# Seven block products for eight in the up projections of the second layer

## The chip, the cores and the metric

The kernel runs on one core of a Trainium2 chip. The metric is the time of one execution in device microseconds (us). The kernel before takes 371.68 us, the median of three runs (371.5 to 371.9).

## The reference

The input `x` is [4, 512, 256] in float32: four batches of 512 tokens with 256 features. Two layers follow each other. Each normalizes `x`, computes a mixer `s` and a gated feed-forward network on the normalized input, and adds `s * silu(ffn)` to `x`. The matrices of the network are `W1` and `W3` [1024, 256] and `W2` [256, 1024].

```python
x = L0_attn_x
xn = _layernorm(x, axis=-1)
s = _L0_attn_ref(xn, ...)            # a product with two small matrices, an RMS norm
g = _silu(_L0_ffn_ref(xn, W1, W2, W3))
x = x + s * g
xn = _layernorm(x, axis=-1)
s = _L1_attn_ref(xn, ...)            # layer norm, causal attention with one head of 256
g = _silu(_L1_ffn_ref(xn, W1, W2, W3))
x = x + s * g

def ffn(x, W1, W2, W3):
    up_gate = einsum('bsd,hd->bsh', x, W1)
    up_lin  = einsum('bsd,hd->bsh', x, W3)
    hidden  = fwht(silu(up_gate) * up_lin)     # a Hadamard transform, a constant matrix
    return einsum('bsh,dh->bsd', hidden, W2)
```

The two einsums with `W1` and `W3` are the up products of which the change speaks.

## The kernel before

Every float32 operand of a large product is held as two float32r tiles, a high part (a rounded copy made by ScalarE) and a low part (the rest, a subtraction on VectorE); the helper `split` (L59 to L62) issues the two. A product is then the sum of three: high by high, low by high and high by low (`mm3`, L64 to L71), all accumulated in one bank of PSUM. Activations are transposed first, so that features lie on partitions; `xTs[layer, b]` holds the pair (high, low), each [128, 2 halves of features, 512 tokens].

The first layer runs over the four batches with `ffn("f0_b")`, and the second with `ffn("f1_b")`; in the profile they appear as `f_0` to `f_3`, both layers under the same names. In `ffn` the 1024 hidden units come in eight chunks `c` of 128. For each chunk there are two banks of tag `gu` (three exist), one for the gate and one for the linear product: 2 x 6 matmuls with 512 moving columns (L411). Then come `silu` on ScalarE (L423), the multiplication on VectorE (L424), a `split` of the result, and with a delay of one chunk the `down` products (L382): 4 tiles of 128 tokens x 3 matmuls with 256 moving columns. Weights `w13` are loaded and split once per layer, in four pairs `q` of two chunks each (`load_w13`, `split_w13`); those of the second layer at L758.

`Beside` interleaves other work: between the parts of a chunk `ffn` calls `slot`, and there the next steps of a list of generators are issued: the gating of the batch before (`gate`), the normalization of the next batch (`norm`), the attention of this batch and the first six steps of that of the next. `attention(b)` begins with the transposition of the normalized input into two banks of tag `ms` (three exist); from these two banks it makes `xTs[1, b]` for the network (L500) and the input of attention itself (L499 to L506).

The Tile framework puts the semaphores in and orders each engine's instructions at build time, from its own estimate of times, with the order of the program as priority. On the chip every engine's queue is executed in that order. All loads of weights and inputs and all stores are issued from SyncE's queue (`SPq`).

Pools of buffers that the change touches: `w13h`, `w13l` (4 each), `xt` (4), `w2` (4), `t4` (10 of [128, 1024]), `hid` (14 of [128, 512]).

## Time and profile before

| | |
|---|---|
| time, median of 3 runs | 371.68 us (371.5 to 371.9) |
| the profiled execution, its own time | 372.08 us |
| its span, first to last instruction | 370.3 us |
| granted TensorE clock | 1.00 |
| TensorE matmul busy | 362.9 us, 98% |
| VectorE busy | 245.7 us, 66% |
| ScalarE busy | 180.1 us, 49% |
| DMA | 15.50 MB, mean 42 GB/s |

The profiled execution is one run; it took 0.40 us more than the median. The profile's views used here are the page with its sums, the timeline of an engine (start, duration, engine, line, operation, tiles), the waits (who waited for whom, in us), the windows (busy time of each engine in a stretch, in the order PE, PEld, DVE, ACT, POOL, then granted clock, DMA share and GB/s) and the list of DMA issues (size and us from issue to landing). PE is TensorE, PEld its weight loads, DVE is VectorE, ACT is ScalarE, SPq SyncE's queue.

### The profile page before, as it was taken

The numbers are of one execution on the slowest core, as the hardware profiler recorded it, in microseconds if no ns is written. First come the engines' busy times: TensorE is split into PE (matmuls) and PEld (weight loads), VectorE is DVE, ScalarE is ACT, GpSimd is POOL, SyncE is SP. The second block draws the span as 40 slices with busy tenths as digits, with TensorE's granted clock in tenths as the row PEclk, the third lists the DMA queues.
The fourth block names the chain that finished last, engine by engine and source line by source line (L and its number), as shares of the span: only waits on it lengthen the run. The fifth ranks groups of instructions, "written<-read, shape, count | busy, mean of one in ns | idle before, by whom it ended". The sixth has DMA issues, their size and how long they took to land.

```text
span 370.3 us, 5487 instructions
## 1 busy us (share of the span) xinstructions
PE 362.9 (98%) x2173; PEld 320.0 (86%) x2173; DVE 245.7 (66%) x520; ACT 180.1 (49%) x332; POOL 18.6 (5%) x22
## 2 busy tenths in 40 slices
PE   7999999999999999999999999999999999999995
PEld 5777998888988898889898998988989899888895
DVE  5998468994539949945958576474774467475543
ACT  3646426163453335545563654274563656366621
POOL 1000111100011102100011000010000000000000
PEclk9999999999999999999999999999999999999999
DMA  7916000300000004110100001100011000010001
GB/s 228 331 60 227 3 0 2 113 0 2 0 2 1 0 19 153 58 57 2 59 2 0 0 2 57 59 0 3 0 58 47 12 0 1 2 57 2 1 2 57
DMA packets 9369, 15.50 MB, mean 42 GB/s; under 512 B 864, under 2 KB 7168, under 8 KB 9344
## 3 DMA queue, kind: packets, MB, share of 16 engines
q1 hardware_dynamic: 9056, 14.90, 12.0%
q8 instruction: 17, 0.28, 0.3%
q10 hardware_dynamic: 288, 0.26, 0.2%
q14 instruction: 8, 0.07, 0.1%
HBM read 13.04 MB, written 2.11 MB: 41 GB/s over the span
## 4 chain that ended last, share of the span: by engine, by line
PE 90%; DVE 3%; DMA 2%; SPq 1%; issue 1%; ACT 1%
PE f_2gu L70 12%; PE f_3gu L70 12%; PE f_1gu L70 12%; PE f_0gu L70 7%; PE f_0dn L382 6%; PE f_2dn L382 6%; PE f_3dn L382 6%; PE f_1dn L382 6%; PE sc L70 4%; PE pv L70 4%; PE o L70 3%; PE v L70 3%; PE tq L70 3%; DMA w13raw<-in_w 2%; PE pt L560 1%; PE mps L170 1%
## 5 line engine op out<-in xcount | busy, mean ns | idle before, releaser
L70 PE MATMUL f_1gu<-xtl,w13h 128*128 128x512 f32 x64 | 25.4, 396 | 0.0
L70 PE MATMUL f_2gu<-xth,w13l 128*128 128x512 f32 x64 | 25.4, 396 | 0.0
L70 PE MATMUL f_3gu<-xtl,w13h 128*128 128x512 f32 x64 | 25.3, 396 | 0.0
L70 PE MATMUL f_2gu<-xtl,w13h 128*128 128x512 f32 x64 | 25.3, 396 | 0.0
L70 PE MATMUL f_1gu<-xth,w13l 128*128 128x512 f32 x64 | 25.3, 396 | 0.0
L70 PE MATMUL f_3gu<-xth,w13l 128*128 128x512 f32 x64 | 25.2, 396 | 0.0
L70 PE MATMUL f_0gu<-xtl,w13h 128*128 128x512 f32 x60 | 23.7, 395 | 0.0
L70 PE MATMUL f_0gu<-xth,w13l 128*128 128x512 f32 x60 | 23.2, 395 | 0.0
L61 ACT CAST f_1hh<-f_1h 128x512 fp32r<-128x512 f32 x16 | 9.9, 621 | 22.4 <-DVE f_1h L424 22.4
L70 PE MATMUL f_3gu<-xth,w13h 128*128 128x512 f32 x64 | 20.7, 400 | 0.0
L70 PE MATMUL f_2gu<-xth,w13h 128*128 128x512 f32 x64 | 20.7, 397 | 0.0
L70 PE MATMUL f_1gu<-xth,w13h 128*128 128x512 f32 x64 | 20.6, 395 | 0.0
L70 PE MATMUL f_0gu<-xth,w13h 128*128 128x512 f32 x60 | 19.7, 410 | 0.6 <-ACT f_0h L423 0.6
L61 ACT CAST f_2hh<-f_2h 128x512 fp32r<-128x512 f32 x16 | 9.9, 619 | 20.2 <-DVE f_2h L424 20.2
L424 DVE TENSOR_TENSOR f_3h<-f_3h,f_3gu 128x512 f32<-128x512 f32 x16 | 11.0, 686 | 10.8 <-PE f_3gu L70 9.5
L382 PE MATMUL f_1dn<-w2h,f_1hh 128*128 128x256 f32 x64 | 17.8, 287 | 0.0
L382 PE MATMUL f_1dn<-w2l,f_1hh 128*128 128x256 f32 x64 | 17.7, 284 | 0.0
L382 PE MATMUL f_3dn<-w2l,f_3hh 128*128 128x256 f32 x64 | 17.7, 281 | 0.0
L382 PE MATMUL f_3dn<-w2h,f_3hh 128*128 128x256 f32 x64 | 17.6, 281 | 0.0
L382 PE MATMUL f_2dn<-w2h,f_2hh 128*128 128x256 f32 x64 | 17.6, 283 | 0.0
L382 PE MATMUL f_2dn<-w2l,f_2hh 128*128 128x256 f32 x64 | 17.5, 281 | 0.0
L424 DVE TENSOR_TENSOR f_2h<-f_2h,f_2gu 128x512 f32<-128x512 f32 x16 | 10.9, 681 | 9.5 <-PE f_2gu L70 8.0
(239 smaller groups left out, 1087.7 us busy)
## 6 DMA issues: line engine op xcount, KB each, us to landing
w13raw<-in_w SPq DMA_DIRECT2D x7, 512.0 KB, 6.1
w2raw<-in_w SPq DMA_DIRECT2D x4, 512.0 KB, 5.4
mrb<-there SPq DMA_DIRECT2D x4, 512.0 KB, 3.7
x<-in_x SPq DMA_DIRECT2D x3, 512.0 KB, 3.3
out<-x SPq DMA_DIRECT2D x6, 256.0 KB, 2.1
w13raw<-in_w SPq DMA_DIRECT2D x2, 256.0 KB, 5.2
wout<-in_w_outT SPq DMA_DIRECT2D x1, 512.0 KB, 9.0
win<-in_w_in SPq DMA_DIRECT2D x1, 512.0 KB, 8.7
```

The costliest lines, as they stand in the source:

```text
L61: h = nc.scalar.copy(hi, src)
L70: ins = nc.tensor.matmul(o, l, r, start=n == 0, stop=n == len(seq) - 1)
L170: nc.tensor.matmul(o[:, i, :], lhsT(k, i), rhs(k), start=k == 0, stop=k == nk - 1)
L382: return nc.tensor.matmul(o, l[:, sl(t)], r[:, c, :], start=start, stop=stop, skip_group_check=True)
L424: gates.append(nc.vector.tensor_tensor(h, h, gu[1], ALU.mult))
L560: nc.tensor.transpose(pt[:, sl(j)], p[:, sl(j)], ident)
```

## The change

The first layer's computation stays. In the second layer the up products of a group `q` (256 hidden units, gate and linear) are read as a product of two 2x2 block matrices: the weights' blocks are (linear, gate) by (first, second half of the features), those of the input (first, second half of the features) by (late, early half of the tokens). Strassen's algorithm in Winograd's form needs seven block products in place of eight, with sums of blocks: S1 to S4 of the weights, T1 to T4 of the input.

- `ffn_s` takes the place of `ffn` for `f1_b`. A group has three banks, `gate_`, `lin` and `z`. Each block product is 6 matmuls with 256 moving columns. Partial results are added by letting further products accumulate on a bank, by three copies on ScalarE (`gate_` into `lin`, `z` into `h1`, `gate_` into `v`) and two additions on VectorE. The down products follow with a delay of one group.
- `prep_s` loads the second layer's raw weights, forms S1 to S4 on VectorE, splits the seven blocks and writes high and low parts to DRAM, 896 KB each per group. It runs beside the first layer's batches 2 (three groups) and 3 (one).
- `load_s` brings the seven blocks of a group back, high and low, for each of the 16 groups of the second layer. Four buffers hold two groups; the load of the next group is issued when a group begins. The resident pairs of L758 are gone.
- `attention` makes the blocks of the input (`t_blocks`): sums T1 to T4 on VectorE, and splits of seven blocks of 256 columns, where before it split two of 512.

The core of the diff (unchanged lines and the code that only gathers buffers are cut):

```diff
@@ split_w13 / norm @@
-        hi = wp.tile([P, 2, S], F32R, tag="w13h", name=f"w13h_{layer}_{q}", bufs=4)
-        lo = wp.tile([P, 2, S], F32R, tag="w13l", name=f"w13l_{layer}_{q}", bufs=4)
+        both = wp.tile([P, 2, 2, S], F32R, tag="w13", name=f"w13_{layer}_{q}", bufs=4)
+        hi, lo = both[:, 0], both[:, 1]
...
+    A11, A12, A22, S1, S2, S3, S4 = range(7)
+    B11, B22, B21, T1, T2, T3, T4 = range(7)
+    sdram = {}
+    def prep_s(q):
+        raw = t4(f"sraw{q}", [P, 4, D])
+        nc.sync.dma_start(raw, a["w13_1"][q])
+        yield
+        sums = t4(f"ssum{q}", [P, 4, D])
...
+        nc.vector.tensor_tensor(s1, a21, a22, ALU.add)
+        nc.vector.tensor_tensor(s3, a11, a21, ALU.subtract)
+        nc.vector.tensor_tensor(s2, s1, a11, ALU.subtract)
+        nc.vector.tensor_tensor(s4, a12, s2, ALU.subtract)
+        yield
+        sdram[q] = there = [
+            dram.tile([P, 7, D], F32, tag=f"s{i}", name=f"s{i}_{q}", bufs=4) for i in range(2)
+        ]
+        for at, n, src in ((0, 3, raw), (3, 4, sums)):
+            parts = [t4(f"sp{at}_{i}_{q}", [P, n, D], F32R) for i in range(2)]
+            split(src[:, :n, :], *parts)
+            for i in range(2):
+                nc.sync.dma_start(there[i][:, at : at + n, :], parts[i].bitcast(F32))
+            yield
+    def load_s(q, n):
+        parts = [
+            wp.tile([P, 7, D], F32R, tag="w13", name=f"sw{i}_{n}_{q}", bufs=4) for i in range(2)
+        ]
+        for i in range(2):
+            nc.sync.dma_start(parts[i].bitcast(F32), sdram[q][i])
+        return parts
...
@@ ffn_s @@
+        for q in range(NH // 2):
+            wh, wl = pairs(q)
+            def product(o, i, j, begin=False, end=False):
+                head = None
+                seq = [(wh, xh), (wl, xh), (wh, xl)]
+                for n, (w, x) in enumerate(seq):
+                    for c in range(2):
+                        with after(head if n == 0 else None):
+                            ins = nc.tensor.matmul(
+                                o[:, c, :], w[:, i, sl(c)], x[j],
+                                start=begin and n + c == 0, stop=end and n == 2,
+                                skip_group_check=True,
+                            )
...
+            gate_, lin = bank(f"{q}g"), None
+            product(gate_, A11, B11, begin=True)
+            lin = bank(f"{q}l")
+            nc.scalar.copy(lin, gate_)
+            z = bank(f"{q}z")
+            product(z, S1, T1, begin=True)
+            h1 = hid(f"{name}h1_{q}").rearrange("p (c n) -> p c n", c=2)
+            nc.scalar.copy(h1, z)
+            slot(4 * q)
+            product(gate_, S2, T2)
+            v = hid(f"{name}v{q}").rearrange("p (c n) -> p c n", c=2)
+            nc.scalar.copy(v, gate_)
+            product(z, S4, B22, end=True)
+            nc.vector.tensor_tensor(v, z, v, ALU.add)
+            slot(4 * q + 1)
+            product(gate_, S3, T3)
+            nc.vector.tensor_tensor(h1, gate_, h1, ALU.add)
+            product(lin, A12, B21, end=True)
+            slot(4 * q + 2)
+            product(gate_, A22, T4, end=True)
+            nc.scalar.activation(h1, h1, AF.Silu)
+            nc.vector.tensor_tensor(h1, h1, v, ALU.mult)
...
+            parts(0, h1)
+            h0 = hid(f"{name}h0_{q}").rearrange("p (c n) -> p c n", c=2)
+            nc.scalar.activation(h0, gate_, AF.Silu)
+            nc.vector.tensor_tensor(h0, h0, lin, ALU.mult)
+            parts(1, h0)
+            queue.append((q, hs))
+            if len(queue) > (1 if last is None else 2):
+                down(*queue.pop(0))
+            slot(4 * q + 3)
...
@@ attention @@
+        os_ = [transpose_half(f"xt1_{b}", xn, k) for k in range(2)]
+        early, late = slice(0, D), slice(D, S)
...
+        b1, b2 = os_
+        nc.scalar.copy(b12, b1[:, early])
+        nc.vector.tensor_tensor(ts_[0], b12, b1[:, late], ALU.subtract)
+        split(b1[:, late], ...)
+        nc.vector.tensor_tensor(ts_[2], b2[:, early], b12, ALU.subtract)
+        nc.vector.tensor_tensor(fs[0], b1, mrb[:, 0, :], ALU.subtract)
+        nc.vector.tensor_tensor(ts_[1], b2[:, early], ts_[0], ALU.subtract)
+        nc.vector.tensor_tensor(ts_[3], b2[:, late], ts_[1], ALU.subtract)
+        split(back, *tb2x)
+        nc.vector.tensor_tensor(fs[1], b2, mrb[:, 0, :], ALU.subtract)
+        split(sums, *tt)
         for k in range(2):
-            o = transpose_half(f"xt1_{b}", xn, k)
-            f = t2(f"xf{b}_{k}", [P, S])
-            nc.vector.tensor_tensor(f, o, mrb[:, 0, :], ALU.subtract)
-            split(o, xh[:, k, :], xl[:, k, :])
+            f = fs[k]
             nc.vector.tensor_tensor(f, f, mrb[:, 1, :], ALU.mult)
...
@@ the loops over batches @@
         if b == 2:
             tasks.append((norm(1, 0), NORM))
+            tasks += [(prep_s(q), 4) for q in range(3)]
         if b == 3:
+            tasks.append((prep_s(3), 4))
...
-    w13_1 = [split_w13(1, q, load_w13(1, q)) for q in range(4)]
+    def pairs(b):
+        def one(q):
+            for n in range(4 * b + q, min(4 * b + q + 2, 16)):
+                if n not in loaded:
+                    loaded[n] = load_s(n % 4, n)
+            return loaded[4 * b + q]
+        return one
...
-            dn = ffn(f"f1_{b}", xTs[1, b], w13_1.__getitem__, w2_1, bg.slot)
+            dn = ffn_s(f"f1_{b}", xTs[1, b], pairs(b), w2_1, bg.slot)
```

More of the change, by code (lines that the diff above doesn't have):

```diff
@@ L271, with xt_pair @@
     xns, xTs, mrs = {}, {}, {}
+    def xt_pair(name):
+        both = act.tile([P, 2, 2, S], F32R, tag="xt", name=name, bufs=2)
+        return both[:, 0], both[:, 1]
+    A11, A12, A22, S1, S2, S3, S4 = range(7)
[6 more added lines that the diff above has]
+        sums = t4(f"ssum{q}", [P, 4, D])
+        a11, a12, a22, a21 = (raw[:, i, :] for i in range(4))
+        s1, s2, s3, s4 = (sums[:, i, :] for i in range(4))
+        nc.vector.tensor_tensor(s1, a21, a22, ALU.add)
[12 more added lines that the diff above has]
+            yield
@@ new lines, in load_s, with t_blocks @@
+    def load_s(q, n):
[5 more added lines that the diff above has]
+        return parts
+    def t_blocks(b):
+        if b % 2:
+            whole = [w2_tile(f"tb{i}_{b}") for i in range(2)]
+        else:
+            whole = [
+                act.tile([P, NH, D], F32R, tag="xt", name=f"tb{i}_{b}", bufs=2)
+                for i in range(2 if b else 1)
+            ]
+        parts = [[w[:, i, :] for i in range(7)] for w in whole]
+        if len(parts) < 2:
+            lo3, lo4 = t4(f"tb3_{b}", [P, 3, D], F32R), t4(f"tb4_{b}", [P, 4, D], F32R)
+            whole = [whole[0], None]
+            parts.append([lo3[:, i, :] for i in range(3)] + [lo4[:, i, :] for i in range(4)])
+            return parts, [(whole[0][:, 0, :], lo3[:, 0, :]),
+                           (whole[0][:, 1:3, :], lo3[:, 1:3, :]),
+                           (whole[0][:, 3:7, :], lo4)]
+        return parts, [tuple(w[:, i:j, :] for w in whole) for i, j in ((0, 1), (1, 3), (3, 7))]
@@ L273, in norm_first @@
     def norm_first():
         xn = act.tile([P, NT, D], F32, tag="xn", name="xn0_0", bufs=3)
-        hi = act.tile([P, 2, S], F32R, tag="xt", name="xth0_0", bufs=4)
-        lo = act.tile([P, 2, S], F32R, tag="xt", name="xtl0_0", bufs=4)
-        xns[0, 0], xTs[0, 0] = xn, (hi, lo)
+        hi, lo = xTs[0, 0] = xt_pair("xt0_0")
+        xns[0, 0] = xn
         x = xs[0]
@@ L326, in norm @@
         xn = act.tile([P, NT, D], F32, tag="xn", name=f"xn{layer}_{b}", bufs=3)
-        hi = act.tile([P, 2, S], F32R, tag="xt", name=f"xth{layer}_{b}", bufs=4)
-        lo = act.tile([P, 2, S], F32R, tag="xt", name=f"xtl{layer}_{b}", bufs=4)
-        xns[layer, b], xTs[layer, b] = xn, (hi, lo)
+        xns[layer, b] = xn
         with after(first["gate"] if layer == 0 and b > 1 else None):
@@ L351, in norm @@
             return
+        hi, lo = xTs[0, b] = xt_pair(f"xt0_{b}")
         for k in range(2):
-            o = transpose_half(f"xt{layer}_{b}", xn, k)
+            o = transpose_half(f"xt0_{b}", xn, k)
             split(o, hi[:, k, :], lo[:, k, :])
@@ L454, in ffn, with ffn_s, down, bank @@
         return None
+    def ffn_s(name, blocks, pairs, w2, slot, last=None):
+        w2h, w2l = w2
+        xh, xl = blocks
+        if last is None:
+            dn = [psum(f"{name}dn{i}", [P, 2, D], tag="dn", bufs=2) for i in range(2)]
+            outs = [dn[t // 2][:, t % 2, :] for t in range(NT)]
+        else:
+            outs = [psum(f"{name}dn{t}", [P, D], **DN[t // 2]) for t in range(NT)]
+        firsts = {}
+        def down(q, hs, tiles=range(NT)):
+            for c in range(2):
+                for t in tiles:
+                    hh, hl = (h[:, c, sl(t % 2)] for h in hs[t // 2])
+                    o = outs[t]
+                    for n, (l, r) in enumerate(((hh, w2h), (hh, w2l), (hl, w2h))):
+                        head = q + c + n == 0
+                        stop = q == NH // 2 - 1 and c == 1 and n == 2
+                        own = head and (t % 2 == 0 or last is not None)
+                        with after(firsts[t // 2] if head and not own else None):
+                            ins = nc.tensor.matmul(
+                                o, l, r[:, 2 * q + c, :], start=own, stop=stop, skip_group_check=True
+                            )
+                        if own:
+                            firsts[t // 2] = ins
+            return ins
+        def bank(n):
+            return psum(f"{name}gu{n}", [P, 2, D], tag="gu", bufs=3)
+        queue = []
+        for q in range(NH // 2):
[4 more added lines that the diff above has]
+                for n, (w, x) in enumerate(seq):
+                    for c in range(2):
+                        with after(head if n == 0 else None):
+                            ins = nc.tensor.matmul(
+                                o[:, c, :], w[:, i, sl(c)], x[j],
+                                start=begin and n + c == 0, stop=end and n == 2,
+                                skip_group_check=True,
+                            )
+                        if head is None:
+                            head = ins
+            gate_, lin = bank(f"{q}g"), None
[20 more added lines that the diff above has]
+            nc.vector.tensor_tensor(h1, h1, v, ALU.mult)
+            hs = []
+            def parts(i, h):
+                hh, hl = (
+                    hid(f"{name}h{p}{i}_{q}", F32R).rearrange("p (c n) -> p c n", c=2) for p in "hl"
+                )
+                split(h, hh, hl)
+                hs.append((hh, hl))
+            parts(0, h1)
[7 more added lines that the diff above has]
+            slot(4 * q + 3)
+        if last is None:
+            for e in queue:
+                down(*e)
+            return dn
+        (q0, q1), ts_ = queue, range(NT)
+        order = [(q0, ts_[:2])] + [(q1, ts_[t : t + 1]) for t in (0, 1)]
+        order += [(q, ts_[t : t + 1]) for t in (2, 3) for q in (q0, q1)]
+        ins = None
+        for q, tiles in order:
+            with after(ins):
+                ins = down(*q, tiles)
+            if q is q1:
+                last(tiles[0], outs[tiles[0]])
+        return None
@@ L493, in attention @@
         xn, wqk, wvo = xns[1, b], first["wqk"], first["wvo"]
-        (xh, xl), mrb = xTs[1, b], mrs[b]
+        mrb = mrs[b]
+        xTs[1, b], (tb11, tb2x, tt) = t_blocks(b)
         xg = gh, gl = t4(f"xgh{b}", [P, 2, S], F32R), t4(f"xgl{b}", [P, 2, S], F32R)
+        os_ = [transpose_half(f"xt1_{b}", xn, k) for k in range(2)]
+        early, late = slice(0, D), slice(D, S)
+        sums = t4(f"tsum{b}", [P, 4, D])
+        ts_ = [sums[:, i, :] for i in range(4)]
+        back = os_[1].rearrange("p (h n) -> p h n", h=2)
+        b1, b2 = os_
+        b12 = t2(f"b12_{b}", [P, D])
+        nc.scalar.copy(b12, b1[:, early])
+        nc.vector.tensor_tensor(ts_[0], b12, b1[:, late], ALU.subtract)
+        split(b1[:, late], tb11[0].rearrange("p a n -> p (a n)") if len(tb11[0].shape) > 2 else tb11[0],
+              tb11[1].rearrange("p a n -> p (a n)") if len(tb11[1].shape) > 2 else tb11[1])
+        nc.vector.tensor_tensor(ts_[2], b2[:, early], b12, ALU.subtract)
+        fs = [t2(f"xf{b}_{k}", [P, S]) for k in range(2)]
+        nc.vector.tensor_tensor(fs[0], b1, mrb[:, 0, :], ALU.subtract)
[4 more added lines that the diff above has]
+        split(sums, *tt)
         for k in range(2):
-            o = transpose_half(f"xt1_{b}", xn, k)
-            f = t2(f"xf{b}_{k}", [P, S])
-            nc.vector.tensor_tensor(f, o, mrb[:, 0, :], ALU.subtract)
-            split(o, xh[:, k, :], xl[:, k, :])
+            f = fs[k]
             nc.vector.tensor_tensor(f, f, mrb[:, 1, :], ALU.mult)
@@ L756, in gate_tile @@
         nc.sync.dma_start(out[B - 1, sl(t), :], x)
-    w13_1 = [split_w13(1, q, load_w13(1, q)) for q in range(4)]
+    loaded = {}
+    def pairs(b):
[5 more added lines that the diff above has]
+        return one
     for b in range(B):
@@ L773 @@
         if b + 1 < B:
-            dn = ffn(f"f1_{b}", xTs[1, b], w13_1.__getitem__, w2_1, bg.slot)
+            dn = ffn_s(f"f1_{b}", xTs[1, b], pairs(b), w2_1, bg.slot)
             bg.finish()
         else:
-            ffn(f"f1_{b}", xTs[1, b], w13_1.__getitem__, w2_1, bg.slot, 4, last=gate_tile)
+            ffn_s(f"f1_{b}", xTs[1, b], pairs(b), w2_1, bg.slot, last=gate_tile)
 def _rows(w):
@@ L788, in _w13, with _w31 @@
     return w.reshape(2, P, 4, S).transpose(2, 1, 0, 3)
+def _w31(w1, w3):
+    g, l = (w.T.reshape(2, P, 4, D) for w in (w1, w3))
+    return np.stack([l[0], l[1], g[1], g[0]], axis=2).transpose(1, 0, 2, 3)
 def _w2(w2):
@@ L822 @@
     for n in range(2):
-        arrays[f"w13_{n}"] = _w13(v[f"L{n}_ffn_W1"], v[f"L{n}_ffn_W3"])
+        arrays[f"w13_{n}"] = (_w31 if n else _w13)(v[f"L{n}_ffn_W1"], v[f"L{n}_ffn_W3"])
         arrays[f"w2_{n}"] = _w2(v[f"L{n}_ffn_W2"])
```

## The prediction

> **What bounds the kernel now.** I read the page's sums first, then the waits of TensorE, then its timeline.

> ```profile
> PE 362.9 (98%) x2173; PEld 320.0 (86%) x2173; DVE 245.7 (66%) x520; ACT 180.1 (49%) x332; POOL 18.6 (5%) x22
> ```

> ```profile
> PE warm L648 <- DVE zr L643: 1.5, 1, 1.5
> PE mps L170 <- ACT wg L198: 0.7, 1, 0.7
> PE f_0gu L70 <- ACT f_0h L423: 0.6, 1, 0.6
> PE f_0gu L417 <- ACT xth L314: 0.4, 1, 0.4
> ```

> TensorE is busy 98% of the span, and the four lines of the second view are all its waits: 3.2 us, all in the first 40 us. Busy time can hide gaps between pipelined matmuls, so the spacing of starts is what I use:

> ```profile
> 168.94 0.28 PE L382 MATMUL f_3dn<-w2h,f_3hh 128*128 128x256 f32 x1
> ...
> 170.35 0.63 PE L70 MATMUL f_3gu<-xth,w13h 128*128 128x512 f32 x2
> ...
> 173.14 0.28 PE L70 MATMUL v<-wvoh,xgh 128*128 128x256 f32 x1
> ```

> Between the first two stand 12 matmuls with 256 columns: 1.41 us, 0.1175 each. Between the second and third stand 12 with 512: 2.79 us, 0.2325 each. TensorE issues without gaps at a time proportional to columns. The second layer runs from about 176 to 366 us; two of its batches by the windows:

> ```profile
> 220.60:269.34 48.74, 48.74 (x303) 43.58 (x302) 30.97 (x68) 25.52 (x46) 2.34 (x2) 1.00 0.07 22
> 269.34:318.00 48.66, 48.66 (x297) 43.21 (x296) 29.93 (x56) 26.33 (x47) 0.00 (x0) 1.00 0.07 23
> ```

> A batch takes 48.7 us, all of it TensorE: 96 x 0.2325 = 22.3 up, 96 x 0.1175 = 11.3 down, and 15.1 of attention. VectorE is busy 62 to 64%, ScalarE 52 to 54%. So less work on TensorE shortens the kernel, as long as the other two can follow.

> **What is removed on TensorE.** A group has 24 matmuls of 512 columns now, 24 x 0.2325 = 5.58 us, and 7 x 6 = 42 of 256 after, 42 x 0.1175 = 4.94. That is 0.645 us less, and over 16 groups 10.3 us. The weights change at every matmul in both forms; the down products do so too at 0.1175, so weight loading adds nothing. [...]

> **ScalarE and VectorE in a group.** Added per group: three copies of [128, 512] on ScalarE and two additions on VectorE (4 and 4 operations of 512 columns become 7 and 6). The nearest rows are casts out of PSUM of 512 columns at 0.59 and additions at 0.69. No row has ScalarE writing PSUM, as `gate_` into `lin` does; I bound it by 0.37 (a 256-column cast) and 0.82 (the slowest 512-column activation, `xg`), and take 0.60, the cast reading the same PSUM. [...] Per batch this is 12 x 0.60 = 7.2 us on ScalarE and 8 x 0.69 = 5.5 on VectorE.

> **The blocks of the input.** ScalarE now casts 2 x 0.59 = 1.2 us per batch; after, 0.37 + 0.37 + 0.59 + 1.05 = 2.4. VectorE has 4 x 0.68 = 2.7; after, five operations of 256 columns at 0.42, three of 512 at 0.68 and one of 1024 at 1.22 make 5.4. The prices of 256 and 1024 columns come from

> ```profile
> L61 ACT CAST w13h<-w13raw 128x1024 fp32r<-128x1024 f32 x7 | 7.4, 1051 | 2.0 <-DMA w13raw<-in_w 2.0
> L62 DVE TENSOR_TENSOR w13l<-w13raw,w13h 128x1024 fp32r<-128x1024 f32 x7 | 8.4, 1217 | 0.0
> L754 DVE TENSOR_TENSOR gl<-gl,xn 128x256 f32<-128x256 f32 x4 | 1.6, 426 | 2.6 <-ACT gl L753 2.4
> ```

> In all, ScalarE goes from 26 to 34.5 us and VectorE from 30.5 to 38.7 us in a batch of 48.7 - 2.6 = 46.1: 75% and 84%. Neither becomes the bound by its sum. The question is waiting.

> **The new waits on TensorE.** Now a bank goes from TensorE to ScalarE once. After, `gate_` goes there and back: the second product on it waits for the copy into `lin`, the third for the copy into `v`, the fourth for VectorE's addition; the second on `z` waits for the copy into `h1`. Four handovers per group, 64 in all, each with the rest of the group, its down products and then the next group queued behind it. A product issues in 6 x 0.1175 = 0.71; its last result lands 0.28 after its start, 0.16 late; a copy takes 0.60. So the second product on `gate_` can start 0.76 us after the first has issued, and the product between them covers 0.71. Three of the four handovers also have a `slot` in between, 15.1 / 16 = 0.94 us of attention on average, and the 24 down products of the group before, 2.82 us, can be ordered into a gap. Cover is short only where ScalarE is away for long, in each softmax:

> ```profile
> 289.90 1.28 ACT L549 ACT_TABLE_LOAD   x1
> ...
> 293.65 1.28 ACT L423 ACT_TABLE_LOAD   x1
> 294.94 0.60 ACT L423 ACTIVATE f_2h<-f_2gu 128x512 f32<-128x512 f32 x1
> ```

> Two table loads with exponentials between them hold ScalarE for up to 5.04 us; copies queued behind wait. Of this 0.61 and 0.27 are casts, so about 4.2. Against 2.82 + 0.94 = 3.76 of cover, some 0.4 us stays open, eight times: 3.2 us. The ends are 0 (the order of the program puts the copies elsewhere) and 1.2 us in each of 16 groups, two handovers each late by one 0.6 us operation: 19.2 us. I take 3.2 because today's trace has the same blocks with ScalarE and shows TensorE no wait in them.

> **The turn of a batch.** This is where it is tight already:

> ```profile
> 264.91 1.04 PE L258 MATMUL xt_2tp<-ident,xn 128*128 128x128 f32 x8
> 268.66 0.58 ACT L61 CAST xth<-xt_2tp 128x512 fp32r<-128x512 f32 x1
> 269.34 0.86 PE L70 MATMUL f_2gu<-xth,w13h 128*128 128x512 f32 x3
> ```

> The first up product starts 0.1 us after the second cast ends; down products and attention filled the 3.4 us before it exactly. VectorE has no gap there from 265.4 to 273.7. The change puts 2.7 us of block sums and 1.2 of additions more into it, and T1, which the second product needs, comes from the last split. Against these 3.9 us stand 12 more down products held back (1.41), and the first and sixth product, 2 x 0.71, which need only early blocks. Left are about 1.0 us; part goes into the following group, so I take 0.8 at each of three turns, 2.4 us, with ends 0 and 3.9 x 3 = 11.7.

> **Streaming the weights.** A group needs 2 x 896 KB, 1.84 MB, each in about 11.5 us: 160 GB/s.

> ```profile
> w13raw<-in_w SPq DMA_DIRECT2D x7, 512.0 KB, 6.1
> x<-in_x SPq DMA_DIRECT2D x3, 512.0 KB, 3.3
> ```

> 3.5 loads of 512 KB at 3.3 us in a row are 11.6 us; at the 331 GB/s of the page's second slice they take 5.5. A load waits for the last product of the group before and is needed a group later. With a group's seven products spread over about 8.5 of its 11.5 us that leaves 14.5 us; in the last batch, whose late groups have little attention, 7.8 + 1.2 = 9. So I cost it at nothing, the cover being one whole group of products; if the cover is gone, it costs up to 2.6 us for each of the last two groups. In SyncE's queue a load can stand behind the transposed moments (`there`, then `mrb`, which waits for it): 1.3 us between their issues now, inside the same slack. Loads also write SBUF beside the engines; subtractions (L62, 512 columns) took 0.68 us at 10 to 22 us, with DMA at 78%, as they do later, so I take nothing.

> **Preparing the sums, the end.** `prep_s` puts per group 4 x 0.42 + 0.93 + 1.22 = 3.8 us on VectorE and 1.85 on ScalarE, beside 98 to 176 us, where they are busy 55.0 and 35.6 of 78.3 us; the four splits at 172 to 180 (1.22 and 1.05 each) go. Cost nothing, hidden by TensorE's own work there; without that cover, 4 x (3.8 - 1.2) = 10.4 us of VectorE. At the end the same 48 down products cover the last chunk's chain: nothing.

> **The sum.** From the profiled execution, 372.08 (span 370.3 and 1.8 around it): -10.3 + 3.2 + 2.4 = 367.4. That run was 0.40 above the median, so 367.0 by the median.

> **The rivals.** *All waits are covered*: 372.1 - 10.3 - 0.4 = 361.4. For it: no wait of TensorE in the second layer today. Against: VectorE at 84%, and the turn.

> *The handovers pace the groups* (the other side): ScalarE's in-order queue holds the copies behind attention's casts and softmax, each group is late by 1.2 us, 19.2 in all: 372.1 - 10.3 + 19.2 - 0.4 = 380.6. It decides from 10.3 / 16 = 0.645 us per group, one operation of ScalarE or VectorE ahead of one handover. For it: the loop gate, copy, gate, copy, gate, addition, gate alone takes 4 x 0.71 + 3 x 0.16 + 0.60 x 2 + 0.69 = 5.2 us of 11.5, and three operations ahead (3 x 0.65) and a softmax (4.2) bring it to 11.4, the group's whole time. Against: the down products wait for nothing in it.

> *The stream comes late*: the second end above, 2 x 2.6 us, on top of my sum: 372.2, no change. For it: 3.3 us per 512 KB today. Against: 331 GB/s when loads are queued.

> That the seven products are not fewer can't be: 43,008 columns per batch against 49,152.

> **Chances.** All covered 0.2; my forecast, 363.5 to 370.9, 0.36, which gives 367.0; no change 0.05 (within 0.2%, 0.74 us, is about what a measurement of this kernel can't tell from none); paced by handovers 0.39, of which a quarter lies above 383. So faster 0.56, same 0.05, slower 0.39, and the range 361.4 to 383.0; the forecast's own is 363.5 to 370.9.

> **What would show it.** Right: 168 up matmuls of 256 columns per batch, 0.1175 apart; batches of 46 to 48 us; TensorE's waits in the second layer 3 to 8 us in sum, named on ScalarE's copies near table loads and on the block splits at the turns; every weight load landed before its first product. Wrong: waits of TensorE on `lin`, `h1`, `v` in most groups (second rival); waits on DMA (third); a spacing above 0.1175 or a granted clock under 1.00 while the stream runs, which no row of this trace can exclude.

## The result and the profile after

The changed kernel takes 398.98 us, the median of four runs (397.1 to 401.08), against 371.79 for the kernel before beside it: 1.0734 times as long, with a 95% interval of 1.0679 to 1.0788. It is 27.2 us slower where 4.7 us less was predicted, and lies above the range. The profiled execution took 401.08 us, its span is 399.3.

The sums and the clock on its page:

```profile
PE 369.2 (92%) x2461; PEld 335.7 (84%) x2461; DVE 280.5 (70%) x592; ACT 212.3 (53%) x392; POOL 18.9 (5%) x22
...
PEclk9999999999999999968999999999999999989998
```

TensorE fell from 98% to 92% of a longer span; VectorE and ScalarE are far from full. The clock row is below 9 from 170 to 190 us, near 355 us and in the last slice; in the kernel before it is not. Was the saving there at all? Two rows of TensorE's timeline, in the middle of the second layer:

```profile
270.78 0.87 PE L565 MATMUL f_1gu2z<-tb,sw 128*128 128x256 f32 x6
271.49 0.28 PE L70 MATMUL pv<-vh,pl 128*128 128x256 f32 x1
```

Six matmuls of 256 columns issue in 0.71 us, as predicted. I added up all spacings of starts in both traces. Spacings at their undisturbed length (0.2325 us for 512 columns, 0.1175 for 256 and so on) sum to 356.8 us before and 346.5 after: the 10.3 us are saved in full. What lies above that length at full clock (the gaps) went from 12.0 to 41.4 us, and another 9.6 us lie in the stretches at half clock. -10.3 + 29.4 + 9.6 = 28.7, and the span grew by 29.0. So nearly everything that went wrong is waiting and clock. Not all of the 9.6 us is the clock itself, because two gaps of 1.2 and 1.5 us lie in these stretches; some 7 us are left for it, an estimate. Who waited, by the waits of TensorE:

```profile
PE pt L750 <- ACT p L739: 3.8, 4, 1.2
PE f_3dn L543 <- ACT f_3hh L61: 2.9, 3, 1.1
PE pv L70 <- ACT ph L61: 2.3, 2, 1.1
PE f_3dn L448 <- DVE f_3hl L62: 1.7, 1, 1.7
PE f_0gu0z L565 <- ACT f_0h L580: 1.7, 1, 1.7
```

No line of this view names a DMA. Of 112 block products only 10 waited for 0.4 us or more, 7.7 us in all; the largest sum is that of `pt`, the transposes of attention's exponentials `p`, an operation that the change doesn't touch. By stage the spacings above their length are 11.9 us at 160 to 200 us, the passage between the layers (6.4 of it at half clock), 16.7 from 200 to 340, and 14.0 from 340 to the end.

**The passage.** Windows of 10 us (columns as in the prediction):

```profile
160.00:170.00 10.00, 9.48 (x56) 8.03 (x54) 9.72 (x32) 4.82 (x14) 1.93 (x2) 1.00 0.88 310
170.00:180.00 10.00, 6.59 (x30) 6.01 (x30) 8.11 (x17) 3.65 (x6) 1.72 (x1) 0.66 0.47 188
180.00:190.00 10.00, 8.14 (x43) 7.01 (x42) 8.18 (x13) 5.96 (x11) 0.00 (x0) 0.83 0.00 0
```

In the kernel before, TensorE is busy for all of these 30 us at clock 1.00 and VectorE for 4.6, 7.1 and 7.4 of 10. Now VectorE is full from 160 to 170 us, and TensorE, which needs its results, starves from 170 us on. Only about 2 us of that is the preparation itself. More is the normalization for the second layer (`norm`), which starts on VectorE at 160.96 us; before, it started at 141.47. The timeline of SyncE's queue tells why the preparation is so late:

```profile
130.69 0.35 SPq L411 DMA_DIRECT2D mrb<-there  x1
131.13 0.37 SPq L294 DMA_DIRECT2D sraw<-in_w  x1
...
158.34 0.38 SPq L294 DMA_DIRECT2D sraw<-in_w  x1
```

The first load of `prep_s` stands right behind the moments of the normalization (`there` at 129.31 us, `mrb`), which wait for their rows until then; the others follow at intervals of 9 us, the last at 158.34. So all the preparation falls into 131 to 175 us, and its last part into the passage. VectorE's timeline shows both ends:

```profile
132.27 0.69 DVE L490 TENSOR_TENSOR f_2h<-f_2h,f_2gu 128x512 f32<-128x512 f32 x1 [4.01 <-PE f_2gu L70]
...
172.93 1.22 DVE L62 TENSOR_TENSOR sp<-ssum,sp 128x1024 fp32r<-128x1024 f32 x1
174.07 0.42 DVE L678 TENSOR_TENSOR tsum<-b,xt_0tp 128x256 f32<-128x256 f32 x1
```

It was idle for 4 us just before, and the last split of the preparation runs directly ahead of the first block sum of the input, for which TensorE waits.

**A softmax.** Timeline of all engines, last batch:

```profile
347.67 0.87 PE L565 MATMUL f_3gu1g<-tb,sw 128*128 128x256 f32 x6
...
348.38 0.87 PE L565 MATMUL f_3gu0g<-tb,sw 128*128 128x256 f32 x6
...
350.10 1.28 ACT L739 ACT_TABLE_LOAD   x1
...
351.90 1.08 PE L750 MATMUL pt<-ident,p 128*128 128x128 f32 x3 [1.03 <-ACT p L739]
```

and the same place of the last batch in the kernel before, where scores end and transposes begin (TensorE and ScalarE):

```profile
332.27 1.28 ACT L549 ACT_TABLE_LOAD   x1
...
332.53 0.28 PE L70 MATMUL sc<-xgh,tql 128*128 128x256 f32 x1
...
334.04 0.37 ACT L549 ACTIVATE p<-sc,neg 128x128 f32<-128x128 f32 x1 [0.49 <-DVE neg L544]
...
337.77 0.27 PE L560 MATMUL pt<-ident,p 128*128 128x128 f32 x1
```

Before, the queue had 5.1 us of products without a wait between scores and transposes, and the table load was over before the exponential's input came. After, it had the two block products shown (1.4 us) and four down products at 350.13, which waited themselves. ScalarE's exponential, 1.28 us of table load late, now meets a TensorE that stands still for 1.2 us. There was something left to do, though: the eight down products that follow `pt` need a VectorE result that was there at 350.80 us. The order made at build time has them behind `pt`, and TensorE ran them after it, the first at 352.63 us.

**The end.** TensorE's timeline, last group:

```profile
384.32 0.98 PE L565 MATMUL f_3gu3z<-tb,sw 128*128 128x256 f32 x6 [0.68 <-ACT f_3h L580]
...
388.84 0.38 PE L543 MATMUL f_3dn<-w2h,f_3hh 128*128 128x256 f32 x1 [1.06 <-ACT f_3hh L61]
```

Here no attention is left. The first line is a bare handover, the wait for the copy of `z`; the second is the wait of the last down products for their group's `silu`, multiplication and cast. The waits of TensorE after 376 us sum to 3.8 us; the kernel before has none in its whole last batch.

### The profile page after: what moved, and what is told of

The parts are those of the page before. It is cut to its first block, busy times and chain, and to the rows that moved or that the text cites. A ratio compares the mean times of both kernels' runs of the same rounds, so it can differ in the third digit from the quotient of the medians.

```text
span 399.3 us, 6257 instructions
## 1 busy us (share of the span) xinstructions
PE 369.2 (92%) x2461; PEld 335.7 (84%) x2461; DVE 280.5 (70%) x592; ACT 212.3 (53%) x392; POOL 18.9 (5%) x22
## 4 chain that ended last, share of the span: by engine, by line
PE 62%; DVE 17%; ACT 10%; DMA 6%; issue 3%; SPq 1%; POOL 0%; ACTq 0%; DVEq 0%
PE f_1gu L70 6%; PE f_2gu L70 5%; DMA sraw<-in_w 4%; PE f_3dn L543 3%; PE sc L70 3%; PE f_0dn L448 3%; PE f_1dn L448 3%; PE v L70 3%; PE tq L70 3%; PE pv L70 3%; PE o L70 2%; PE f_1dn L543 2%; PE f_2dn L543 2%; DMA w13raw<-in_w 2%; ACT L739 2%
## 5 line engine op out<-in xcount | busy, mean ns | idle before, releaser
L70 PE MATMUL f_2gu<-xt,w 128*128 128x512 f32 x96 | 24.6, 394 | 0.0
L70 PE MATMUL f_3gu<-xt,w 128*128 128x512 f32 x96 | 24.6, 395 | 0.0
L70 PE MATMUL f_1gu<-xt,w 128*128 128x512 f32 x96 | 24.4, 394 | 0.0
L70 PE MATMUL f_0gu<-xt,w 128*128 128x512 f32 x84 | 21.6, 406 | 1.2 <-ACT f_0h L489 1.2
L61 ACT CAST f_2hh<-f_2h 128x512 fp32r<-128x512 f32 x16 | 9.9, 621 | 22.2 <-DVE f_2h L490 18.1
L70 PEld LDWEIGHTS f_0gu<-xt,w 128*128 128x128 f32 x84 | 15.5, 188 | 5.9 <-ACT f_0h L489 1.6
L70 PEld LDWEIGHTS f_1gu<-xt,w 128*128 128x128 f32 x96 | 17.2, 188 | 3.3
L70 PEld LDWEIGHTS f_2gu<-xt,w 128*128 128x128 f32 x96 | 17.2, 188 | 3.2
L70 PEld LDWEIGHTS f_3gu<-xt,w 128*128 128x128 f32 x96 | 17.2, 188 | 3.2
L61 ACT CAST f_1hh<-f_1h 128x512 fp32r<-128x512 f32 x16 | 10.0, 622 | 15.2 <-DVE f_1h L490 12.0
L61 ACT CAST f_3hh<-f_3h 128x512 fp32r<-128x512 f32 x16 | 9.9, 618 | 11.9 <-DVE f_3h L490 7.2
L62 DVE TENSOR_TENSOR f_2hl<-f_2h,f_2hh 128x512 fp32r<-128x512 f32 x16 | 10.9, 684 | 4.2 <-ACT f_2hh L61 4.2
L62 DVE TENSOR_TENSOR f_3hl<-f_3h,f_3hh 128x512 fp32r<-128x512 f32 x16 | 11.0, 687 | 4.1 <-ACT f_3hh L61 4.0
L62 DVE TENSOR_TENSOR f_1hl<-f_1h,f_1hh 128x512 fp32r<-128x512 f32 x16 | 10.9, 683 | 3.0 <-ACT f_1hh L61 3.0
L70 PE MATMUL o<-mh,xt 128*128 128x256 f32 x64 | 12.5, 283 | 0.0
L61 ACT CAST f_0hh<-f_0h 128x512 fp32r<-128x512 f32 x12 | 7.4, 619 | 8.8 <-DVE f_0h L607 3.9
L62 DVE TENSOR_TENSOR f_0hl<-f_0h,f_0hh 128x512 fp32r<-128x512 f32 x12 | 8.2, 686 | 5.2 <-ACT f_0hh L61 5.1
L70 PEld LDWEIGHTS o<-mh,xt 128*128 128x128 f32 x64 | 10.5, 191 | 0.3
L70 PE MATMUL pv<-vh,pl 128*128 128x256 f32 x40 | 10.5, 287 | 0.4 <-DVE pl L62 0.3
## 6 DMA issues: line engine op xcount, KB each, us to landing
s<-sp SPq DMA_DIRECT2D x8, 512.0 KB, 5.0
w2raw<-in_w SPq DMA_DIRECT2D x4, 512.0 KB, 7.2
mrb<-there SPq DMA_DIRECT2D x4, 512.0 KB, 4.2
sraw<-in_w SPq DMA_DIRECT2D x4, 512.0 KB, 4.9
w13raw<-in_w SPq DMA_DIRECT2D x3, 512.0 KB, 8.0
x<-in_x SPq DMA_DIRECT2D x3, 512.0 KB, 3.5
```

The costliest lines, as they stand in the source:

```text
L61: h = nc.scalar.copy(hi, src)
L62: return h, engine.tensor_tensor(lo, src, hi.bitcast(F32), ALU.subtract)
L70: ins = nc.tensor.matmul(o, l, r, start=n == 0, stop=n == len(seq) - 1)
```

## The experiments

The theories: *handovers* (a product waits until ScalarE or VectorE has read its bank, and TensorE's fixed order has nothing else to put there), with the rival *load* (the two engines merely have more to do); *preparation* (`prep_s` ahead of the passage); *table loads*; *stream*. Every time is a median against the kernel before on the same chip, which took 371.5 to 371.8 us. One thing goes with nearly every edit: the Tile framework orders the instructions anew, so an edit changes the order in places that it doesn't touch. Only `e5_exp` and `e7_no_stream` keep the order of the changed kernel, and `e6_exp_before` that of the kernel before.

### One cause taken away at a time

**No preparation** (`e1_no_prep`).

```diff
-            tasks += [(prep_s(q), 4) for q in range(3)]
-            tasks.append((prep_s(3), 4))
+        if b == 1:
+            tasks += [(stand_in(q), 1) for q in range(4)]  # DMAs of split weights to sdram[q]
```

> Leaves out the preparation of the weight sums beside the first layer: no raw load, no sums, no splits; in their place the first layer's split weights are stored to the same DRAM tiles early, beside batch 1, so that the second layer's computation runs on other weights at the same size. Stream, handovers and block sums of the input stay. In the changed kernel's profile the gaps between matmuls, against before, are 11.9 us at the passage between the layers (160 to 200 us), 16.7 in the batches (200 to 340) and 14.0 at the end. Theory A, the handovers pace the groups: the passage is a small part of it, 396 to 399 us. Theory B, the preparation clogs VectorE, the t4 buffers and the DMA engines before the second layer and so holds the first blocks of the input back: the passage's 11.9 us go, 386 to 389 us, and the clock keeps 1.00 there. Theory C, table loads on ScalarE that the built order doesn't reckon with: no change, 398 to 399.

Measured: 384.2 us (1.0337 [1.0322, 1.0352]), 14.8 less, clock 1.000. A window of the passage:

```profile
170.00:180.00 10.00, 10.00 (x78) 9.59 (x77) 3.86 (x7) 4.21 (x9) 0.00 (x0) 1.00 0.31 104
```

TensorE is full again in these 10 us and VectorE more than half empty; from 180 to 190 us TensorE is busy for 8.38. No matmul runs at half clock, and `norm` starts at 141.21 us again. The preparation is a cause of its own; the gain is 1.8 us larger than its theory allowed at most, and where it lies is told with `f1_early`.

**Handovers of 8 columns** (`e2_small`).

```diff
-            nc.scalar.copy(lin, gate_)
+            nc.scalar.copy(tiny[:, :, 0:8], gate_[:, :, 0:8])
...
-            nc.vector.tensor_tensor(h1, gate_, h1, ALU.add)
+            nc.vector.tensor_tensor(tiny[:, :, 8:16], gate_[:, :, 0:8], tiny[:, :, 8:16], ALU.add)
```

> Every handover stays, but its operation has 8 of 256 columns per half: three small copies on ScalarE and two small additions on VectorE per group, into a scratch tile. The copy into lin is no longer added to (lin starts fresh), the gate is made from z, and silu reads PSUM. So the waits of TensorE on the same engines stay and their time on the engines nearly goes (about 0.2 us in place of 0.6 each). Theory A in the form of work on the engines (12 x 0.4 us of ScalarE and 8 x 0.45 of VectorE per batch, and queues behind it): 383 to 388 us. Theory A in the form of the round trip itself: 393 to 397. Theories B and C: 393 to 398.

Measured: 383.3 us (1.0294 [1.0248, 1.0341]), 15.6 less. The waits before `pt` fell from 6.1 to 1.5 us of spacing; the passage stayed. This is the value expected if the length of the operations costs, and the queues behind them; a round trip as such was expected to leave 393 or more. Yet the next run, without any handover, is another 11.7 us faster.

**No copies, no additions** (`e3_no_hand`): the same without the five lines.

> The three copies and the two additions of each group are left out altogether: gate, z and lin are accumulated by the same seven products, silu reads z and the gate from PSUM, both are multiplied by lin. No handover inside a group; matmuls, stream, preparation and block sums of the input stay. Theory A: the 16.7 us of the batches and most of the end's 14.0 go, 372 to 376 us. Theory B: the passage's 11.9 us stay, and where nothing else costs, 380 to 385. Theory C: the waits for softmax stay as they are (6.05 us before the transposes of p, 2.8 before the products with values), 388 to 392.

Measured: 371.7 us (1.0006 [0.9994, 1.0018]), 27.3 less. The waits of `pt` on `p` are gone, although ScalarE still loads its tables 16 times in the second layer. Without the preparation they had stayed (4.1 us in `e1_no_prep` against 3.8), so they go with the handovers.

**An exponential for silu** (`e5_exp`), to be rid of the table loads (16 of 1.28 us in the second layer of the changed kernel); and as a control **the same in the kernel before** (`e6_exp_before`).

```diff
-            nc.scalar.activation(h1, h1, AF.Silu)
+            nc.scalar.activation(h1, h1, AF.Exp, scale=0.01)
```

> The changed kernel with exp(0.01 x) in place of silu everywhere, so that ScalarE has one table and the 16 loads of 1.28 us go; nothing else, the order of every engine is the same. Theory C: each of eight softmaxes gains 1.3 to 2.6 us, 383 to 388 us. Theory A: less queueing on ScalarE, some 0.5 us per softmax, 393 to 396. Theory B: 397 to 399.

> Control: the kernel before with an exponential of a small multiple in place of every silu, so no table loads in either layer. Theory handovers: in the kernel before nothing waits for ScalarE, so the table loads are hidden, 371.0 to 372.0 us (no change), while the same edit took 11.0 us from the changed kernel. If table loads cost by themselves: 8 or more us less.

Measured: 388.0 us (1.0431 [1.0407, 1.0454]), 11.0 less; in the kernel before 371.8 (1.0004 [0.9995, 1.0014]), no change. By its number the first run meets the theory of table loads (383 to 388) at its edge, and since the order is the same, the 11.0 us are theirs alone. But the same loads are free in the kernel before, and in `e3_no_hand` nothing waits for `p`: they are not a cause of their own but a delay that the handovers have exposed.

**No stream** (`e7_no_stream`): two groups are loaded once and used for all.

```diff
-            for n in range(4 * b + q, min(4 * b + q + 2, 16)):
+            for n in range(2):
...
-            return loaded[4 * b + q]
+            return loaded[q % 2]
```

> The changed kernel that loads the block sums of two groups once and uses these two pairs for all 16 groups, so 14 of 16 loads of 2 x 896 KB are left out. Theory stream (late loads, or loads that slow the engines down): 390 or less. Handovers and preparation as the causes: no change but for the clock, 396 to 400.

Measured: 398.6 us (1.0754 [1.0712, 1.0797]), the same. The stream is hidden.

### Load or order, and both causes together

**Copies and additions off the products' path** (`e4_load`): same number and size, but issued after the last product, on banks that no further product of the group writes.

```diff
             product(gate_, A22, T4, end=True)
+            nc.scalar.copy(h1, z)
+            nc.scalar.copy(v, lin)
+            nc.scalar.copy(v, z)
+            nc.vector.tensor_tensor(h1, z, h1, ALU.add)
+            nc.vector.tensor_tensor(v, z, v, ALU.add)
```

> The changed kernel in which the three copies and two additions of a group stay in number and size, but are issued after the group's products and read banks that no later product of the group writes, so no product waits for them. Theory handovers: the time falls nearly as without copies and additions, 371 to 376 us. Theory load (ScalarE and VectorE are too full, whoever waits): it stays above 383. With the chain silu to down products longer by the copies, one group of delay still covers it, so nothing of that is expected.

Measured: 375.3 us (1.0107 [1.0091, 1.0122]). Against no copies at all the load costs 3.7 us; that products wait for it costs 23.6 (398.98 - 375.34), the new order included. The window from 200 to 345 us, of this kernel:

```profile
200.00:345.00 145.00, 142.04 (x1129) 138.07 (x1128) 108.87 (x235) 99.75 (x182) 4.03 (x4) 1.00 0.49 176
```

and of the changed kernel:

```profile
200.00:345.00 145.00, 135.55 (x1051) 128.97 (x1050) 104.86 (x225) 92.92 (x169) 4.03 (x4) 1.00 0.43 160
```

VectorE and ScalarE are busier here (108.9 and 99.8 against 104.9 and 92.9 us), yet TensorE is busy 6.5 us more. The rival *load* falls as the main cause; 3.7 us are left to it.

**Neither preparation nor handovers** (`e8_both`): the first and the third edit together.

> The changed kernel without the preparation of the block sums (stand-ins are written to DRAM early, from split weights of the first layer) and without copies and additions in a group. If handovers and preparation are the two causes and nothing else costs, the time is that of the forecast without them: the span before of 370.3 less 10.3 of products, about 360 us of span and 362 of time; if the two savings seen one by one (14.8 and 27.3) simply add up, 356.9. If a third cause is left (streaming, the sums of the input, the clock), 366 or more, and the gaps that remain show where.

Measured: 363.7 us (0.9788 [0.9773, 0.9802]), 7.9 less than the kernel before. So the 10.3 us are to be had on TensorE, and the two causes make 35.3 of the 37.5 us between a full gain and the result. One by one they give 14.8 and 27.3; 6.8 us of that is common. Where it lies is seen by batches, in the table below.

### Can it be repaired, and which handovers count

**Early preparation** (`f1_early`), the whole computation.

```diff
+            tasks.append((prep_s(0), 4))                      # batch 1
-            tasks.append((norm(1, 0), NORM))                  # batch 2
-            tasks += [(prep_s(q), 4) for q in range(3)]
+            tasks += [(prep_s(q), 4) for q in range(1, 4)]
+            tasks.append((norm(1, 0), NORM))
-            tasks.append((prep_s(3), 4))                      # batch 3
```

> The whole computation; the preparation of the block sums is moved: group 0 to the first layer's batch 1, groups 1 to 3 to batch 2 ahead of the normalization for the second layer (so its loads stand ahead of the transposed moments in SyncE's queue), none in batch 3. Theory preparation (it costs because it lies before the passage, not because of its amount): 384 to 389 us, nearly the 384.2 of the kernel without it, and TensorE without half clock at 165 to 185 us. If the amount of work on VectorE is the cause: 395 or more, with waits of TensorE near 60 to 135 us in place of those at the passage.

Measured: 386.7 us (1.0408 [1.0389, 1.0426]), 12.3 less. SyncE's timeline:

```profile
70.78 0.33 SPq L294 DMA_DIRECT2D sraw<-in_w  x1
...
124.28 0.38 SPq L294 DMA_DIRECT2D sraw<-in_w  x1
...
134.08 0.34 SPq L409 DMA_DIRECT2D there<-rows  x1
```

The same work, loaded from 71 to 124 us and ahead of the moments, costs only 2.5 us more than none. It was its place, not its amount; `norm` starts at 145.51 us here.

But place is more than the passage. This is what lies above the undisturbed spacing of TensorE's matmuls in the second layer, by batch, each from its first block product on and the first with the passage before it (us in the profiled executions; in brackets the part at half clock):

| | first | second | third | last |
|---|---|---|---|---|
| changed kernel | 17.7 (6.4) | 7.2 | 3.6 | 14.1 (3.2) |
| `e1_no_prep` | 8.5 | 5.3 | 3.1 | 8.3 |
| `f1_early` | 8.5 | 5.3 | 3.1 | 9.6 (1.4) |
| `e3_no_hand` | 8.3 (2.2) | 2.4 | 1.1 | 2.0 |
| `e8_both` | 1.6 | 1.2 | 1.0 | 1.8 |

Without the preparation 17.4 us go in these executions (14.8 by the medians): 9.2 at the passage and in the first batch, and 5.8 in the last batch, some 160 us after the preparation is done. From the second batch on, the matmuls of `e1_no_prep` and `f1_early` come in the same order, tile by tile, and those of the changed kernel in another. So part of what the preparation costs is the order that was built around it. How much of the 5.8 us is order and how much the clock is open. In the last batch, too, lies most of what the two causes have in common: without handovers its gaps are short with the preparation (2.0) and without it (1.8).

**Pieces of down products ahead of waiting products** (`f2_pinned`).

```diff
-            product(gate_, S3, T3)
+            product(gate_, S3, T3, behind=piece(0, 1))   # 6 down products first; so for S4, A22
```

> As the kernel with the early preparation, and the 24 down products of the group before are cut into four pieces of 6 (0.71 us each), three of them fixed ahead of the block products that wait for a copy or an addition (S4 on z, S3 and A22 on gate_). Theory handovers wait because too little stands between: 3 to 6 us less than with the early preparation alone, 379 to 385. Theory the built order puts the cover right already, and what is late is ScalarE behind its table loads and the transposes of p: within 1 us of the early preparation alone, or slower by the lost freedom.

Measured: 386.5 us (1.0402 [1.038, 1.0423]), the same as `f1_early`. The two traces have the same 2461 matmuls in the same order of tiles, and the same order on ScalarE and VectorE: the built program had these pieces there already, and the pins moved nothing. So the run repeats `f1_early`; whether more cover would help stays open.

**tanh for silu** (`f3_tanh`), and **all three repairs** (`f4_all`).

```diff
-            nc.scalar.activation(h0, gate_, AF.Silu)
-            nc.vector.tensor_tensor(h0, h0, lin, ALU.mult)
+            nc.scalar.activation(h0, gate_, AF.Tanh, scale=0.5)
+            nc.vector.scalar_tensor_tensor(h0, h0, 1.0, gate_, ALU.add, ALU.mult)
+            nc.vector.scalar_tensor_tensor(h0, h0, 0.5, lin, ALU.mult, ALU.mult)
```

> As the kernel with the early preparation, and the second layer's silu is written as a/2 (1 + tanh(a/2)), with tanh in place of silu, so that it may share its table with the exponential; one more VectorE operation for each silu (0.69 us, 10 per batch, 6.9 us). Theory table loads (11.0 us less when silu was replaced by an exponential): 374 to 380 us, no table loads inside the second layer, no waits on p. If VectorE becomes too full by it (from 72% to 86% of the middle of the second layer): 382 or more.

> Early preparation, pieces of down products ahead of the waiting block products, and tanh for silu together. If their gains add: 370 to 377 us. The copies and additions stay, which as mere load cost 3.7 us (375.3 against 371.7), so below 367 it can't get by this reckoning: 363.7 without copies and preparation, and 3.7.

Measured: 397.5 us (1.0694 [1.0669, 1.0719]) and 398.3 (1.071 [1.0686, 1.0734]). A miss: 10.7 us slower than `f1_early`, although the table loads inside the second layer are gone and no wait of `pt` on `p` is left among TensorE's. `f4_all` has the instructions of `f3_tanh` in the same order, so it is a repeat as well. The waits of ScalarE, with tanh:

```profile
ACT f_1th L594 <- DVE f_1h L589: 8.4, 4, 3.7
...
ACT f_0gu1l L576 <- DVE f_0h L609: 4.6, 1, 4.6
```

In `f1_early` ScalarE waited 3.9 us for the additions in the first of these places. The longer VectorE chain holds back even the copy into `lin` (the second line). I read this as a ring of three in-order engines that got longer and so outweighed what the table loads had cost; the order was built anew here too, and no run separates the two.

**Which handovers**, on the early preparation: only the last batch cut to 8 columns (`g1_last`), only ScalarE's copies (`g2_copies`), only VectorE's additions (`g3_adds`), all (`g4_all_small`); the edits are those of `e2_small`.

> Early preparation (386.7 us); only in the last of the second layer's four batches are the copies and additions cut to 8 columns per half. If handovers cost the same in each batch: a quarter of what cutting all of them saves, some 4 us less, 382 to 383. If the last batch pays most because no attention is left to fill its waits (gaps of about 7 us after 360 us in the kernel with early preparation): 377 to 380.

> Early preparation; ScalarE's three copies per group are cut to 8 columns per half, VectorE's two additions keep their size (with another tile as second operand). Theory ScalarE (its queue holds copies behind table loads and casts, and its load brings p late): most of the gain of cutting both, 371 to 376 us. Theory VectorE: 383 to 386.

> Early preparation; VectorE's two additions per group are cut to 8 columns per half, ScalarE's copies keep their size. Theory ScalarE: 382 to 386 us. Theory VectorE: 371 to 376.

> Early preparation; all five handovers of a group stay in place and in order, cut to 8 columns per half. From the same cut on the changed kernel (399.0 to 383.3, 15.6 us) and from early preparation (12.3): 371 if the two add. Down to 366 if handovers this short leave no wait at all (363.7 was measured without copies, additions and preparation).

Measured, against 386.7: 385.3 (-1.4), 378.9 (-7.8), 384.2 (-2.5) and 369.3 (-17.4). Copies count three times as much as additions: `g3_adds` lies where the theory ScalarE had it, `g2_copies` 2.9 us above. Another 7.1 us go only when both are short, as in a ring where one long link is enough; but each of these runs has an order of its own, so the shares are rough. The last batch gave less than a quarter, against both expectations: in its profile 2.5 us are lost to gaps from 360 us on instead of 5.8, but at 330 to 350 us 3.4 instead of 2.2, and there 2.9 more at half clock, where `f1_early` has none. What the end costs by itself stays open.

No version here does the whole computation faster than the kernel before. With early preparation and the copies at their mere load, an estimate of what can be reached is 363.7 + 3.7 = 367.4 us, or 369.9 with the 2.5 us that the early preparation still costs: 2 to 4 us below the kernel before. How to free the products of the copies without more VectorE work was not found.

## Why the prediction was wrong

- **Saving on TensorE, 10.3 us: right**, 356.8 to 346.5 us of undisturbed issue, and 7.9 us faster in fact once both causes are out.
- **Prices of the operations: right.** ScalarE's copy from PSUM to PSUM, bounded by 0.37 and 0.82 and taken as 0.60, took 0.57 to 0.61; to SBUF 0.58 to 0.62: writing PSUM was no slower here. Additions took 0.66 to 0.69.
- **Stream, nothing: right**; loads landed in 5.5 us, no wait on a DMA, 398.6 without them.
- **Turn of the batch, 2.4 us: near in size, by luck.** Around the first products of the batches, at 231, 284 and 333 us, only the first shows gaps above 0.4 us (0.7, 0.9 and 0.5), and the first two wait for VectorE's additions, not for the block splits that I had priced. The block splits are waited for where the sum had nothing, at the passage: 0.8 and 1.2 us.
- **Preparing the sums, "Cost nothing": the first step that failed**, by 12.3 us of place (the order built around it included) and 2.5 of work. I compared its 15 us on VectorE with the idle time from 98 to 176 us, and named 10.4 us as the price if cover is gone. But the sum of idle time does not say when the work can begin: its loads stood behind `there` and `mrb` in SyncE's queue until 131 us, though I had named that queue for the stream. And the passage has a deadline that a mean hides: `norm` came 19.5 us later, and TensorE ran out of work.
- **The new waits, 3.2 us: the second step that failed.** Measured are 20.5 us (384.2 to 363.7), or 17.4 on the early preparation, near the upper end of 19.2 that I had given. The argument "today's trace has the same blocks with ScalarE and shows TensorE no wait in them" was the error: before, 5.1 us of products that wait for nobody stood between scores and transposes, and the change makes just those products wait. I counted the down products and attention as cover, and they do fill most handovers; but then they are used up, or ordered elsewhere, where attention needed cover itself.
- **The rival "the handovers pace the groups"**, 380.6 us, had nearly the size (its 19.2 against 20.5), but not the sign I gave for it, waits in most groups: 10 of 112 block products waited for 0.4 us or more. The waits show on `pt`, `pv` and the down products, so the near size is in part luck.
- **The end, nothing: wrong**, by the 3.8 us of waits in its timeline; what it costs by itself the runs leave open.
- **The clock**: a granted clock below 1.00, which I named as something no row could exclude, did appear, and cost some 7 us in the profiled execution. It is a small part of the miss: the four executions had clocks of 0.979 to 0.996, and the one with 0.996 still took 397.1 us.

Wrong, then: one term missing (the preparation's place, 12.3 us), one term five to six times too small (the handovers), and a small loss of clock that came with them.

## What to carry to other kernels

The kernel before, with TensorE at 98%, lived on products that wait for nobody, 5.1 us of them at the softmax shown; before splitting such products into pieces that go to another engine and back, ask what covers the slow places of the other work afterwards, not only what covers the new waits. Work that "fits into idle time" needs its start looked up: which queue issues its first load, what stands ahead of it there, and which deadline lies behind it. Moving five operations off the products' path was worth 23.6 us, making room on the engines 3.7. And where a framework orders the instructions, compare the order of two builds before calling an edit local: here the pins changed no order at all, and a change to early work changed the order of the last batch.

## What the runs showed of the hardware

```profile
169.32 0.28 PE L448 MATMUL f_3dn<-w2l,f_3hh 128*128 128x256 f32 x1
171.34 0.41 PE L448 MATMUL f_3dn<-w2h,f_3hl 128*128 128x256 f32 x1 [1.74 <-DVE f_3hl L62]
171.56 0.40 PE L448 MATMUL f_3dn<-w2h,f_3hh 128*128 128x256 f32 x1
```

After a gap of 1.9 us beyond the usual spacing, matmuls of 256 columns take 0.41 instead of 0.28 us and start 0.21 apart instead of 0.12; from 172 to 178 us the granted clock is 0.50. The half-clock stretches of this trace lasted 6.8, 3.4, 3.4 and 3.4 us, apart from the last microsecond, and none of the gaps from 169 to 185 us was longer than 1.9 us. Gaps of 1.0 and 1.2 us within 3 us came before the fall at 352 us.

But neither the length of the gaps nor their sequence decides it in these runs. `e5_exp`, with the same order of matmuls, had gaps of 1.9, 1.8 and 1.4 us from 169 to 178 us at full clock and fell only at 183 us, after one more of 1.9. `g2_copies` fell at 286 us after a gap of 1.4 us with one of 0.5 before it, and `g4_all_small` kept its clock, 1.000 over the profiled execution, after one of 1.8 at 358 us. The kernel without preparation, whose gaps after 40 us are 1.3 us at most, kept a clock of 1.000. What decides is not shown here.
